# FFN inner and outer products on 32x32 places of TensorE, one expert to a place, without the mask

## Chip, cores and metric

One core of a Trainium2 chip. The metric is device time in microseconds, the median of the runs shown. Three runs of the kernel before took 2077.69 (median), 2072.56 and 2080.45 us. The profiled execution took 2074.38 us, of which the span from the first to the last instruction is 2072.3.

## What is computed

The input x is 10000 rows of 512. A graph layer comes first: layernorm, messages over 5000 edges summed by destination, two matrix products with batchnorm and silu, and the result added to x. The FFN follows, and the change is in it alone. Cut to what matters:

```python
grouped = x.reshape(B, S // t, t, D)                      # t = 16 tokens to a group, D = 512
cont_logits = einsum('bgtd,des->bgtes', grouped, controller) + tie
cont_perm = (cont_logits == max(cont_logits, over t))     # per group, each of 64 (e, s) picks one token
inner = einsum('bgtesf,bgtes->bgesf', einsum('bgtd,desf->bgtesf', grouped, f1), cont_perm)
inter2 = einsum('bgesf,esfd->bgesd', relu(inner), f2)     # f = 32
result = einsum('bgesd,bgtes->bgtd', inter2, cont_perm)
```

So 64 experts (16 x 4 pairs e, s) each take one token of every group of 16, multiply it by a 512x32 matrix of their own, take relu, multiply by a 32x512 matrix of their own, and give the sum back to that token. Everything is f32.

## The kernel before

The graph layer takes the first 1240 us or so and is untouched. The FFN walks the 10000 rows in 20 chunks of 512 tokens (the last has 272). A chunk has G = 32 groups. It goes through four steps of a pipeline, and `step` (L695) holds, for one turn, the work of four chunks in an order written by hand: chunk `a` is normalized and gets its logits and choice, chunk `b` gathers and does the inner product, chunk `d` the outer product, chunk `e` scatters to the output; `nxt` is the chunk that is loaded. A scheduler interleaves neighbours slightly (the first gather with the residual transposes, outer with the logits), and each engine then runs its own queue in order.

What the stages do in a turn, by line:

- `by_token` (L581) turns the choice of `b` into one-hot columns; DVE makes the mask `bd` from it (L587).
- `residual` (L523 to L526) and `norm` (L532 to L539) prepare rows of `a`; `flip` (L547, L549) transposes them, `logits` (L557) multiplies by the controller and `choose` (L570 to L573) finds the maxima on DVE.
- `gather(k)` (L602), for each quarter k of the 512 features, multiplies the normalized rows with the one-hot mask: for each expert and group, the chosen token's features, in the two `pb` buffers of PSUM. ACT copies both to `gs` (L608).
- `inner(k)` (L623) multiplies `gs` by f1. A stationary operand holds 64 columns, that is two experts of 32, and the moving operand the 64 columns of the same two experts' tokens (32 groups each). So each product has four blocks of 32x32, of which two are an expert with its own tokens and two are an expert with the other's tokens. Four k are summed in PSUM, in `pi`.
- `relu` (L630) takes relu of all of `pi` on DVE and multiplies by the mask `own` (1 for the wanted blocks, 0 for the others) into `ib`.
- `outer(u)`, u = 0 to 3 (L645), multiplies `ib` by f2: 64 rows (two experts) by 64 columns, on four places of the array. A half `i` of u fills one `pb` buffer, and is copied into `it` at once, by DVE (L651) for the first half of u = 0 and 1, by ACT (L653) for the others.
- `turn` (L659) is eight 32x32-wise transposes of `it` on DVE, `split` (L668) makes the scatter's mask on GpSimd, `scatter` (L686) multiplies both back to tokens, again in `pb`, and DVE adds the result to the rows (L692), which then go out.

[...]`ps` two of one bank, `pb` two buffers of two banks each, and `pi` one buffer of two banks, which the logits use too. The two `pb` buffers are handed round between gather, outer and scatter, so a matmul that takes a buffer waits for the copy or the addition that reads it last. f2 is loaded by eight DMAs before the first turn.

Of the kernel before, what the change touches and what calls it, by code (L numbers as in the profile page):

```python
# [35 lines left out]
G = CH // T  # L36
# [14 lines left out]
def gnn_ffn_kernel(ctx: ExitStack, tc: tile.TileContext, a: dict, out: bass.AP):  # L51
    nc = tc.nc
# [10 lines left out]
    const = ctx.enter_context(tc.tile_pool(name="const", bufs=1))  # L63
# [114 lines left out]
    with tc.tile_pool(name="pe1", bufs=1) as pe1, tc.tile_pool(name="pe", bufs=2) as pe, \  # L178
# [48 lines left out]
        for t in range(NTE):  # L227
            nc.gpsimd.indirect_dma_start(
                out=xgs[t], out_offset=None, in_=x,
# [3 lines left out]
        for g in range(NTE // EG):  # L233
# [9 lines left out]
            for i in range(EG):  # L243
                r = row[:, :i + 1, :]
                d = dst_f[:, g * EG + i:g * EG + i + 1]
# [3 lines left out]
                                               op0=ALU.is_equal, op1=ALU.mult, accum_out=count[:, i:i + 1])  # L249
# [21 lines left out]
            for i in range(EG):  # L271
                t = g * EG + i
# [6 lines left out]
            for i in range(EG):  # L279
                pc = ps_e.tile([TE, H], F32, name="pc", bufs=3)  # L280
                for k in range(i, EG):
                    nc.tensor.matmul(pc, lhsT=same[k][:, i, :], rhs=xgs[g * EG + k], start=(k == i),  # L282
                                     stop=(k == EG - 1))
                nc.scalar.copy(xgs[g * EG + i], pc)
                sums.append(tc.keep_in_program_order(nc.gpsimd.indirect_dma_start(
                    out=views[i], out_offset=bass.IndirectOffsetOnAxis(ap=to_i[:, i:i + 1], axis=0),
                    in_=xgs[g * EG + i], in_offset=None, compute_op=ALU.add)))
# [116 lines left out]
    with tc.tile_pool(name="pb", bufs=1) as pb, tc.tile_pool(name="ps_3", bufs=1, space=PSUM) as ps_3:  # L404
        u2 = weight_sums(pb, "w2", w2, 4, H // 2)
        for o, i in enumerate([NP - 1, *range(NP - 1)]):
            if o > 0:
# [4 lines left out]
                for m in range(4):  # L412
                    for r in range(2):
                        h = pieces[m][:, r].rearrange("p t n -> p (t n)")
                        nc.scalar.activation(h, h, AF.Silu, bias=sh1[:, 4 * r + m:4 * r + m + 1],
                                             scale=sc1[:, 4 * r + m:4 * r + m + 1])
            else:
                for r, t in ((0, 0), (1, 1), (1, 0), (0, 1)):
                    for m in range(4):
                        h = pieces[m][:, r, t, :]  # L420
# [3 lines left out]
            for m in range(2):  # L424
# [3 lines left out]
                for r in range(2):  # L428
                    for t in range(2):
                        nc.vector.bn_stats(out=st2[:, 2 * r + m, 2 * i + t, :], in_=h2[:, r, t, :])  # L430
                nc.sync.dma_start(out=h2s.rearrange("p (r m) n -> p m r n", r=2)[:, m, :, 2 * i * TB:2 * (i + 1) * TB],
                                  in_=h2.rearrange("p r t n -> p r (t n)"))
# [5 lines left out]
    ctl = const.tile([P, KH, 2, ES // 2], F32, name="ctl")  # L438
# [4 lines left out]
    for h in range(2):  # L443
        nc.sync.dma_start(out=tie[h * ES:(h + 1) * ES, :], in_=a["c_tie"])

    own = const.tile([P, 2, G], F32, name="own")
    nc.vector.memset(own, 0.0)
    for r in range(4):
        nc.vector.memset(own[32 * r:32 * r + 32, r % 2, :], 1.0)

    gmask = load_const("c_gmask", [P, 8])
    odd_p = const.tile([P, 2], F32, name="odd_p")
    nc.vector.tensor_reduce(odd_p, gmask.rearrange("p (q h) -> p h q", h=2), AX.X, ALU.add)
# [5 lines left out]
    HD = H // 2  # L459
    wf = ctx.enter_context(tc.tile_pool(name="wf", bufs=1))  # L460
    f1_sb = wf.tile([P, KH, ES * F], F32, name="f1_sb")
    f2_sb = wf.tile([P, MF, H], F32, name="f2_sb")
    pf = ctx.enter_context(tc.tile_pool(name="pf", bufs=2))
    ps_s = ctx.enter_context(tc.tile_pool(name="ps_s", bufs=2, space=PSUM))
    ps_b = ctx.enter_context(tc.tile_pool(name="ps_b", bufs=2, space=PSUM))
    ps_i = ctx.enter_context(tc.tile_pool(name="ps_i", bufs=1, space=PSUM))

    class Chunk:

# [82 lines left out]
        def logits(self, k, xlt):  # L552

            if k == 0:
                self.pl = ps_i.tile([P, 2, CH], F32, name="pi")
            for h, (o, n) in enumerate(self.halves):
                nc.tensor.matmul(self.pl[h * ES:(h + 1) * ES, 0, :n], lhsT=ctl[:, k].rearrange("p h j -> p (h j)"), rhs=xlt[:, o:o + n],  # L557
                                 start=(k == 0), stop=(k == KH - 1), skip_group_check=True)

        def choose(self):  # L560

            self.perm = pf.tile([P, CH // 2], F32, name="perm", bufs=5)
            mx = pf.tile([P, G // 2], F32, name="mx")
            if not self.full:
                nc.vector.memset(self.perm, 0.0)
            for s, n in [(slice(0, P), CH // 2)] if self.full else [
                    (slice(h * ES, (h + 1) * ES), n) for h, (_, n) in enumerate(self.halves)]:
                k, g = s.stop - s.start, n // T
                lg = self.perm[s, :n].rearrange("e (g t) -> e g t", t=T)
                nc.vector.tensor_add(lg, self.pl[s, 0, :n].rearrange("e (g t) -> e g t", t=T),  # L570
                                     tie[s, None, :].to_broadcast([k, g, T]))
                nc.vector.tensor_reduce(mx[s, :g], lg, AX.X, ALU.max)
                nc.vector.tensor_tensor(lg, lg, mx[s, :g, None].to_broadcast([k, g, T]), ALU.is_equal)  # L573
# [39 lines left out]

        def inner(self, k, gs):


            if k == 0:
                self.pi = ps_i.tile([P, MF, 2 * G], F32, name="pi")
            gs = gs.rearrange("p (h j) g -> p h j g", h=2)
            for m in range(MF):  # L620
                for q in range(2):
                    j = 4 * (m // 2) + 2 * q + m % 2
                    nc.tensor.matmul(self.pi[64 * q:64 * q + 64, m, :], lhsT=f1_sb[:, k, 2 * F * j:2 * F * (j + 1)],  # L623
                                     rhs=gs[:, :, j, :],
                                     start=(k == 0 and m % 8 == 0), stop=(k == KH - 1), skip_group_check=True)

        def relu(self):

            self.ib = pf.tile([P, MF, 2 * G], F32, name="ib")
            nc.vector.scalar_tensor_tensor(self.ib, self.pi, 0.0, own.rearrange("p h g -> p (h g)")[:, None, :]  # L630
                                           .to_broadcast([P, MF, 2 * G]), op0=ALU.max, op1=ALU.mult)

        def outer(self, u):


            if u == 0:
                self.it = pf.tile([P, HD // 2, 32, 2], F32, name="it", bufs=1)
            for i in range(2):
                b = 2 * u + i
                po = ps_b.tile([P, 2, 2, HD], F32, name="pb")  # L640
                for t in range(2):
                    for dh in range(2):
                        for q in range(2):
                            s = slice(64 * q, 64 * q + 64)
                            nc.tensor.matmul(po[64 * dh:64 * dh + 64, q, t, :], lhsT=self.ib[s, 2 * b + t, :],  # L645
                                             rhs=f2_sb[s, 2 * b + t, HD * dh:HD * (dh + 1)], start=True, stop=True,
                                             skip_group_check=True)
                dst = self.it[:, :, 4 * b:4 * b + 4, :].rearrange("p d c l -> p c d l")
                src = po.rearrange("p q t (d l) -> p (q t) d l", l=2)
                if i == 0 and u < 2:  # L650
                    nc.vector.tensor_copy(dst, src)  # L651
                else:
                    nc.scalar.copy(dst, src)  # L653
# [128 lines left out]
        chunks[c].silu()  # L782
    nc.sync.dma_start(out=f1_sb, in_=a["L0_ffn_f1"].rearrange("(k p) n -> p k n", p=P))

    f2 = a["L0_ffn_f2"].rearrange("(b q t h f) d -> q h f b t d", h=2, q=2, t=2, f=F)
    f2_to = f2_sb.rearrange("p (b t) d -> p b t d", t=2)
    for q in range(2):
        for h in range(2):
            for t in range(2):
                rows = slice(64 * q + F * h, 64 * q + F * (h + 1))  # L790
                nc.sync.dma_start(out=f2_to[rows, :, t, :], in_=f2[q, h, :, :, t, :])
    for c in range(NC + 3):
        step(at(c), at(c - 1), at(c - 2), at(c - 3), at(c + 1))

# [60 lines left out]
```

## Time and profile before

| | us |
|---|---|
| median of three runs | 2077.69 |
| profiled execution | 2074.38 |
| its span | 2072.3 |
| graph layer, to the FFN's first chunk choice | about 1270 |
| FFN turns with all four chunks, most of them | 37.0 to 37.2 each |
| PE busy in the turn from 1500 to 1537 | 35.06 |
| DVE, ACT, GpSimd busy there | 22.13, 18.93, 9.81 |
| mean granted TensorE clock, whole span | 0.948 |

In a profile row of a group, the columns are line, engine, operation, output and inputs by name, then the count, the busy time, the mean duration of one in ns, and the idle time before it with what ended it. A row of the timeline has the start in us, the length of the merged stretch, then engine and line, the count, and in square brackets the idle time before it with its cause. A row of windows has, for each engine, busy time and number of instructions, then the granted clock, the share of the DMA engines and GB/s. Busy times of PE overlap, since matmuls on different places of the array run at once; so the distance between starts says more than the duration of one.

### The profile page before, as it was taken

The numbers are of one execution on the slowest core, as the hardware profiler recorded it, in microseconds if no ns is written. First come the engines' busy times: TensorE is split into PE (matmuls) and PEld (weight loads), VectorE is DVE, ScalarE is ACT, GpSimd is POOL, SyncE is SP. The second block draws the span as 40 slices with busy tenths as digits, with TensorE's granted clock in tenths as the row PEclk, the third lists the DMA queues.
The fourth block names the chain that finished last, engine by engine and source line by source line (L and its number), as shares of the span: only waits on it lengthen the run. The fifth ranks groups of instructions, "written<-read, shape, count | busy, mean of one in ns | idle before, by whom it ended". The sixth has DMA issues, their size and how long they took to land.

```text
span 2072.3 us, 38292 instructions
## 1 busy us (share of the span) xinstructions
PE 1858.1 (90%) x16562; PEld 1041.7 (50%) x16562; DVE 1145.5 (55%) x1860; ACT 726.4 (35%) x969; POOL 626.7 (30%) x630
## 2 busy tenths in 40 slices
PE   7935499999999989999999996899989999999984
PEld 3412244444444434444444444576666676666662
DVE  9723267777777774334333442265565565665655
ACT  3412233333333333222222203454454554545422
POOL 7144433333333324222233313023222122222311
PEclk9967699999999999999999997899999999999987
DMA  9986444444444122322333209222222222222110
GB/s 354 359 176 87 110 181 157 160 161 159 161 160 160 80 80 119 139 119 119 126 132 120 118 40 253 73 83 76 91 83 94 75 82 94 93 75 83 34 39 35
DMA packets 95119, 256.01 MB, mean 124 GB/s; under 512 B 7767, under 2 KB 8357, under 8 KB 94374
## 3 DMA queue, kind: packets, MB, share of 16 engines
q1 hardware_dynamic: 85990, 232.58, 30.7%
q0 software_dynamic: 8960, 20.98, 5.0%
q8 instruction: 130, 2.13, 0.4%
q14 instruction: 39, 0.32, 0.0%
HBM read 143.47 MB, written 110.07 MB: 122 GB/s over the span
## 4 chain that ended last, share of the span: by engine, by line
PE 66%; DVE 13%; DMA 7%; ACT 6%; POOL 5%; issue 3%; SPq 0%; DVEq 0%; POOLq 0%; ACTq 0%
PE x L133 9%; PE z L133 9%; PE pi L623 7%; PE pb L645 7%; PE v L133 5%; PE w L133 5%; PE pb L602 5%; PE pb L686 4%; PE pc L282 3%; PE y L133 3%; PE pi L557 2%; DVE ln_st L329 2%; DMA yt<-h2s 2%; ACT xt L341 2%; PE pt L133 2%
## 5 line engine op out<-in xcount | busy, mean ns | idle before, releaser
L133 PE MATMUL x<-h_s,w_u 128*128 128x500 f32 x640 | 289.5, 585 | 0.6 <-ACT s L138 0.3
L653 ACT COPY it<-pb 128x1024 f32<-128x1024 f32 x120 | 121.8, 1050 | 256.5 <-PE pb L645 256.5
L645 PE MATMUL pb<-f_sb,ib 64*64 64x256 f32 x2560 | 191.1, 390 | 11.1 <-DVE x L692 8.4
L133 PEld LDWEIGHTS x<-h_s,w_u 128*128 128x128 f32 x640 | 122.3, 191 | 148.8 <-issue 142.4
L659 DVE STREAM_TRANSPOSE it<-it 128x1024 f32<-128x1024 f32 x160 | 186.9, 1212 | 11.3 <-ACT it L653 11.3
L608 ACT COPY gs<-pb 128x1024 f32<-128x1024 f32 x152 | 153.1, 1065 | 101.6 <-PE pb L602 101.6
L623 PE MATMUL pi<-gs,f_sb 128*64 128x64 f32 x5120 | 178.5, 232 | 5.2 <-issue 5.2
L623 PEld LDWEIGHTS pi<-gs,f_sb 128*64 128x64 f32 x5120 | 167.4, 146 | 20.6 <-issue 14.1
L602 PE MATMUL pb<-bd,xl 32*128 32x128 f32 x2504 | 143.6, 302 | 35.8 <-ACT gs L608 26.9
L668 POOL TENSOR_TENSOR pv<-perm,odd_t 64x512 f32<-64x512 f32 (+1 forms) x80 | 99.7, 1246 | 222.0 <-PE pb L686 194.1
L133 PE MATMUL z<-h_s,w 128*128 128x500 f32 x320 | 148.0, 585 | 3.3 <-POOL h_s L123 3.3
L143 DVE SCALAR_TENSOR_TENSOR t<-w,s 128x500 f32<-128x500 f32 x60 | 40.7, 678 | 190.5 <-PE w L133 186.7
L602 PEld LDWEIGHTS pb<-bd,xl 32*128 32x128 f32 x2504 | 115.4, 196 | 60.7 <-ACT gs L608 38.8
L133 PE MATMUL z<-h_s,w_u 128*128 128x500 f32 x320 | 143.9, 583 | 0.0
L645 PEld LDWEIGHTS pb<-f_sb,ib 64*64 64x64 f32 x2560 | 95.3, 134 | 88.6 <-issue 29.7
L123 POOL TENSOR_TENSOR h_s<-hc 128x500 f32<-128x500 f32 x60 | 77.0, 1319 | 148.7 <-PE z L133 148.7
L532 POOL TENSOR_SCALAR ln_rs<-ln_mv 128x4 f32<-128x4 f32 (+2 forms) x22 | 4.9, 224 | 373.4 <-DVE ln_mv L526 363.7
L138 ACT COPY s<-z 128x500 f32<-128x500 f32 x60 | 34.5, 575 | 219.2 <-PE z L133 150.2
L692 DVE TENSOR_TENSOR x<-pb,x 128x1024 f32<-128x1024 f32 (+1 forms) x40 | 48.2, 1208 | 101.9 <-PE pb L686 101.9
L686 PE MATMUL pb<-it,pv 64*32 64x256 f32 x2504 | 81.7, 395 | 20.8 <-DVE it L659 20.8
L348 PE MATMUL pt<-ident,xt 125*128 125x125 f32 x320 | 47.9, 288 | 56.6 <-DVE xt L342 47.8
L341 ACT ACTIVATE xt<-xt,ln_sh,ln_rs 125x512 f32<-125x512 f32 x80 | 59.6, 805 | 110.4 <-POOL ln_sh L336 110.4
(174 smaller groups left out, 3078.8 us busy)
## 6 DMA issues: line engine op xcount, KB each, us to landing
h1s<-h SPq DMA_DIRECT2D x36, 1000.0 KB
agg<-zero SPq DMA_DIRECT2D x10, 2048.0 KB
xt<-in_x_dram SPq DMA_DIRECT2D x20, 1000.0 KB
at<-agg SPq DMA_DIRECT2D x20, 1000.0 KB
hc<-h1s SPq DMA_DIRECT2D x20, 1000.0 KB
h2s<-h SPq DMA_DIRECT2D x20, 1000.0 KB
x<-in_x_dram SPq DMA_DIRECT2D x39, 512.0 KB
out_dram<-x SPq DMA_DIRECT2D x39, 512.0 KB
```

Of the source, the lines that this page charges most:

```text
L123: eng.tensor_tensor(t[:, k0:k1], q(*x0, k0, k1), q(*x1, k0, k1), op)
L133: nc.tensor.matmul(bank, lhsT=us[n][:, k, m * P:(m + 1) * P], rhs=bs[n][k], start=start and k == 0, stop=k == kb - 1, skip_group_check=True)
L282: nc.tensor.matmul(pc, lhsT=same[k][:, i, :], rhs=xgs[g * EG + k], start=(k == i), stop=(k == EG - 1))
L341: nc.scalar.activation(r, r, AF.Identity, bias=self.sh[:RT, j, :], scale=self.rs[:RT, j, :])
L602: nc.tensor.matmul(pg[r // 2][:, r % 2, j], lhsT=self.xl[j][s, k * P:(k + 1) * P], rhs=self.bd[s, j], start=True, stop=True)
L608: nc.scalar.copy(to[:, 8 * i:8 * i + 8], pg[i].rearrange("d r j e h -> d (r j) e h"))
L623: nc.tensor.matmul(self.pi[64 * q:64 * q + 64, m, :], lhsT=f1_sb[:, k, 2 * F * j:2 * F * (j + 1)], rhs=gs[:, :, j, :], start=(k == 0 and m ...
L645: nc.tensor.matmul(po[64 * dh:64 * dh + 64, q, t, :], lhsT=self.ib[s, 2 * b + t, :], rhs=f2_sb[s, 2 * b + t, HD * dh:HD * (dh + 1)], start ...
L653: nc.scalar.copy(dst, src)
L659: nc.vector.transpose(it, it)
L668: nc.gpsimd.tensor_tensor(self.pv[dh * ES:(dh + 1) * ES, :, o:o + n].rearrange("e v (q t) -> e v q t", q=q), self.perm[i * ES:(i + 1) * ES ...
L686: nc.tensor.matmul(pr[32 * r:32 * r + 32, dh, j % 2, :], lhsT=self.pv[s, v, tok], rhs=self.it[s, :, 2 * (4 * r + j) + v, :], start=(v == 0 ...
```

## The change

Inner and outer work on one expert at a time, 32 rows and 32 columns each. `inner` issues 64 matmuls per k instead of 32, each with 32 stationary and 32 moving columns, on the four column places in turn; no product of an expert with another's tokens is formed, so the mask `own` is gone, `relu` is a plain maximum over half as many elements, and `pi` is half as wide. `pi` is one bank now and has two buffers. `outer(u)` issues 32 matmuls instead of 16, on 16 places (four of rows, four of columns), takes both `pb` buffers at its start and fills their four banks, one bank to a row place; the innermost loop goes over the row places, so every second pair of matmuls is in the second buffer. After all 32, DVE copies the first buffer and ACT the second, for every u. The rows of f2 are laid out to fit, by 16 DMAs of half the size.

```diff
-    own = const.tile([P, 2, G], F32, name="own")
-    nc.vector.memset(own, 0.0)
-    for r in range(4):
-        nc.vector.memset(own[32 * r:32 * r + 32, r % 2, :], 1.0)
...
-    ps_i = ctx.enter_context(tc.tile_pool(name="ps_i", bufs=1, space=PSUM))
+    ps_i = ctx.enter_context(tc.tile_pool(name="ps_i", bufs=2, space=PSUM))
...
-                self.pl = ps_i.tile([P, 2, CH], F32, name="pi")
+                self.pl = ps_i.tile([P, CH], F32, name="pi")
...
             if k == 0:
-                self.pi = ps_i.tile([P, MF, 2 * G], F32, name="pi")
-            gs = gs.rearrange("p (h j) g -> p h j g", h=2)
+                self.pi = ps_i.tile([P, MF, G], F32, name="pi")
+            gs = gs.rearrange("p (h j) g -> p j h g", h=2)
             for m in range(MF):
-                for q in range(2):
-                    j = 4 * (m // 2) + 2 * q + m % 2
-                    nc.tensor.matmul(self.pi[64 * q:64 * q + 64, m, :], lhsT=f1_sb[:, k, 2 * F * j:2 * F * (j + 1)],
-                                     rhs=gs[:, :, j, :],
-                                     start=(k == 0 and m % 8 == 0), stop=(k == KH - 1), skip_group_check=True)
+                for r in range(4):
+                    j, h = 8 * (m // 4) + 2 * r + m % 4 // 2, m % 2
+                    nc.tensor.matmul(self.pi[32 * r:32 * r + 32, m, :], lhsT=f1_sb[:, k, F * (2 * j + h):F * (2 * j + h + 1)],
+                                     rhs=gs[:, j, h, :], start=(k == 0 and m == 0), stop=(k == KH - 1),
+                                     skip_group_check=True)
...
-            self.ib = pf.tile([P, MF, 2 * G], F32, name="ib")
-            nc.vector.scalar_tensor_tensor(self.ib, self.pi, 0.0, own.rearrange("p h g -> p (h g)")[:, None, :]
-                                           .to_broadcast([P, MF, 2 * G]), op0=ALU.max, op1=ALU.mult)
+            self.ib = pf.tile([P, MF, G], F32, name="ib")
+            nc.vector.tensor_scalar(self.ib, self.pi, 0.0, None, op0=ALU.max)
...
+            po = [ps_b.tile([P, 2, 2, HD], F32, name="pb") for _ in range(2)]
+            for t in range(2):
+                for h in range(2):
+                    for dh in range(2):
+                        c = 64 * dh + 32 * h
+                        for r in range(4):
+                            s = slice(32 * r, 32 * r + 32)
+                            m = 4 * u + 2 * t + h
+                            nc.tensor.matmul(po[r // 2][c:c + 32, r % 2, t, :], lhsT=self.ib[s, m, :],
+                                             rhs=f2_sb[s, m, HD * dh:HD * (dh + 1)], start=True, stop=True,
+                                             skip_group_check=True)
             for i in range(2):
-                b = 2 * u + i
-                po = ps_b.tile([P, 2, 2, HD], F32, name="pb")
-                for t in range(2):
-                    for dh in range(2):
-                        for q in range(2):
-                            s = slice(64 * q, 64 * q + 64)
-                            nc.tensor.matmul(po[64 * dh:64 * dh + 64, q, t, :], lhsT=self.ib[s, 2 * b + t, :],
-                                             rhs=f2_sb[s, 2 * b + t, HD * dh:HD * (dh + 1)], start=True, stop=True,
-                                             skip_group_check=True)
-                dst = self.it[:, :, 4 * b:4 * b + 4, :].rearrange("p d c l -> p c d l")
-                src = po.rearrange("p q t (d l) -> p (q t) d l", l=2)
-                if i == 0 and u < 2:
+                dst = self.it[:, :, 8 * u + 4 * i:8 * u + 4 * i + 4, :].rearrange("p d c l -> p c d l")
+                src = po[i].rearrange("p q t (d l) -> p (q t) d l", l=2)
+                if i == 0:
                     nc.vector.tensor_copy(dst, src)
                 else:
                     nc.scalar.copy(dst, src)
...
-    for q in range(2):
-        for h in range(2):
-            for t in range(2):
-                rows = slice(64 * q + F * h, 64 * q + F * (h + 1))
-                nc.sync.dma_start(out=f2_to[rows, :, t, :], in_=f2[q, h, :, :, t, :])
+    for u in range(4):
+        for r in range(4):
+            nc.sync.dma_start(out=f2_sb[32 * r:32 * r + 32, 4 * u:4 * u + 4, :], in_=f2[u, r])
```

More of the change, by code (lines that the diff above doesn't have):

```diff
@@ L554, in logits @@
             if k == 0:
-                self.pl = ps_i.tile([P, 2, CH], F32, name="pi")
+                self.pl = ps_i.tile([P, CH], F32, name="pi")
             for h, (o, n) in enumerate(self.halves):
-                nc.tensor.matmul(self.pl[h * ES:(h + 1) * ES, 0, :n], lhsT=ctl[:, k].rearrange("p h j -> p (h j)"), rhs=xlt[:, o:o + n],
-                                 start=(k == 0), stop=(k == KH - 1), skip_group_check=True)
+                nc.tensor.matmul(self.pl[h * ES:(h + 1) * ES, :n], lhsT=ctl[:, k].rearrange("p h j -> p (h j)"),
+                                 rhs=xlt[:, o:o + n], start=(k == 0), stop=(k == KH - 1), skip_group_check=True)
         def choose(self):
@@ L569, in choose @@
                 lg = self.perm[s, :n].rearrange("e (g t) -> e g t", t=T)
-                nc.vector.tensor_add(lg, self.pl[s, 0, :n].rearrange("e (g t) -> e g t", t=T),
+                nc.vector.tensor_add(lg, self.pl[s, :n].rearrange("e (g t) -> e g t", t=T),
                                      tie[s, None, :].to_broadcast([k, g, T]))
@@ L783, in gnn_ffn_kernel @@
     nc.sync.dma_start(out=f1_sb, in_=a["L0_ffn_f1"].rearrange("(k p) n -> p k n", p=P))
-    f2 = a["L0_ffn_f2"].rearrange("(b q t h f) d -> q h f b t d", h=2, q=2, t=2, f=F)
-    f2_to = f2_sb.rearrange("p (b t) d -> p b t d", t=2)
-    for q in range(2):
-        for h in range(2):
-            for t in range(2):
-                rows = slice(64 * q + F * h, 64 * q + F * (h + 1))
-                nc.sync.dma_start(out=f2_to[rows, :, t, :], in_=f2[q, h, :, :, t, :])
+    f2 = a["L0_ffn_f2"].rearrange("(u r b f) d -> u r f b d", u=4, r=4, f=F)
+    for u in range(4):
+        for r in range(4):
+            nc.sync.dma_start(out=f2_sb[32 * r:32 * r + 32, 4 * u:4 * u + 4, :], in_=f2[u, r])
     for c in range(NC + 3):
```

## The prediction

> **What bounds the kernel now.** I read the page, then one step of the FFN stage in order of time, then its windows, and last the single matmul records. The page puts PE on top, with the two lines that the change rewrites:
>
> ```profile
> PE 1858.1 (90%) x16562; PEld 1041.7 (50%) x16562; DVE 1145.5 (55%) x1860; ACT 726.4 (35%) x969; POOL 626.7 (30%) x630
> ...
> L645 PE MATMUL pb<-f_sb,ib 64*64 64x256 f32 x2560 | 191.1, 390 | 11.1 <-DVE x L692 8.4
> ...
> L623 PE MATMUL pi<-gs,f_sb 128*64 128x64 f32 x5120 | 178.5, 232 | 5.2 <-issue 5.2
> ```
>
> Inner (L623) and outer (L645) hold PE for 370 us. Every f32 matmul of the program stands in the trace as two, so I count passes. A full step lasts 37.0 to 37.2 us in most of its turns. The timeline of the one from 1499.82 to 1536.84 shows what ends each wait of PE:
>
> ```profile
> 1508.51 2.04 ACT L608 COPY gs<-pb 128x1024 f32<-128x1024 f32 x2
> ...
> 1509.63 0.49 PE L602 MATMUL pb<-bd,xl 32*128 32x128 f32 x4 [0.55 <-ACT gs L608]
> 1510.61 1.16 PE L602 MATMUL pb<-bd,xl 32*128 32x128 f32 x28 [0.48 <-ACT gs L608]
> 1511.70 2.08 PE L623 MATMUL pi<-gs,f_sb 128*64 128x64 f32 x64
> 1511.85 2.11 ACT L608 COPY gs<-pb 128x1024 f32<-128x1024 f32 x2
> 1513.71 1.45 PE L602 MATMUL pb<-bd,xl 32*128 32x128 f32 x32
> 1515.10 2.09 PE L623 MATMUL pi<-gs,f_sb 128*64 128x64 f32 x64
> 1517.11 1.96 PE L686 MATMUL pb<-it,pv 64*32 64x256 f32 x64
> 1521.02 1.96 PE L686 MATMUL pb<-it,pv 64*32 64x256 f32 x64
> 1522.91 1.09 PE L645 MATMUL pb<-f_sb,ib 64*64 64x256 f32 x16
> 1523.09 1.22 DVE L692 TENSOR_TENSOR x<-pb,x 128x1024 f32<-128x1024 f32 x1 [0.73 <-PE pb L686]
> 1524.37 1.09 PE L645 MATMUL pb<-f_sb,ib 64*64 64x256 f32 x16 [0.36 <-DVE x L692]
> ```
>
> PE is full but for about 1 us at 1509 to 1511: gather(2) waits for the ACT copies that free the two pb buffers. Gather(3) starts at 1513.71 and needs the copy that ends at 1513.96. So the first two inners run in the shade of ACT. Inner(2) and inner(3) do not, and outer doesn't either.
>
> The last view is the clock. Two windows, the second with one drop to half speed:
>
> ```profile
> 1500.00:1537.00 37.00, 35.06 (x691) 24.96 (x691) 22.13 (x30) 18.93 (x23) 9.81 (x12) 1.00 0.27 88
> 1537.00:1574.00 37.00, 32.80 (x644) 24.34 (x647) 20.85 (x27) 16.08 (x20) 9.81 (x12) 0.95 0.28 87
> ```
>
> That step took 40.55 us.
>
> **How matmuls pack.** In the records, passes on different places of the array start 6 to 7 ns apart, then a gap follows until the places are free: L623 starts two in 58.5 ns, L645 four in 216, L686 eight in 218. A full-array 128x500 pass takes 418 ns, so a column costs 0.83 ns, and 64 columns 53, 256 columns 213. Each round is one stream plus about 5 ns.
>
> **The change, part by part, for one full step.**
> - Inner: 128 passes of 32 columns per k, four column places. A stream is 27 ns, four starts 26. A round is about 33 ns, 32 rounds make 1.05, and with the 0.15 that lies between a block's rounds and the next block 1.2 us; now it is 2.01 (1515.10 to 1517.11). Gain 0.8 each. For inner(0) and inner(1) it is nothing: gather(2) and (3) wait for ACT in any case. For inner(2) and (3) it is 1.6.
> - Is that rate sustained? The Trainium skill ("TensorE: Matmul & The Clock Gate", Part 1, section "Wait — 56ns, not 53.3ns?") says that starts never come closer than about 25 ns. By that, an inner takes 128 x 25 = 3.2 us and the change loses. Against it stand the rounds of 6 to 7 ns, but L686 averages 25 ns, so no row shows more than a burst. In L686's later rounds, the last weight loads come 17 ns apart for every two passes, as if just decoded: 8.5 ns a pass. I take that (34 ns a round) and keep 25 for the range.
> - Outer: 64 passes per u on 16 places instead of 32 on four. Four rounds of 218 would be 0.87. But L686's late loads read as a queue of about 64 entries; 16 places with two passes, each a load and a matmul, fill it, and the second half comes late. I take 1.4 us, between 0.87+0.2 and the present 1.88 (1532.49 to 1534.37).
> - Both pb buffers at once. The program's order has the third matmul of outer(u) on the second buffer, so all wait for both evictions. Outer(0): now 2.48 from start to flips (two halves of 1.05 and the wait); then 1.25 (L692 after scatter(1)) + 1.4 = 2.65, +0.15. Outer(1), with flips and lo(0): 4.2 becomes 3.9, -0.3. Outer(2): 4.8 becomes 4.3, -0.5. Outer(3): lo(3) covers 0.6 of the 1.4 that a DVE copy (1.22) takes to come free, so lo(3), 0.8 of stall and 1.4 of work, and by_token 0.15 later for choose: 2.95 against 2.47, +0.5.
> - Evictions: of the eight copies of a step DVE takes four instead of two (1.22 each, from L651's rows), ACT four instead of six (1.05, L653). One has a victim: DVE's copy of outer(3) now stands between choose and bd. bd (now 0.48 after by_token) waits till about 1.3, and the first gather with it: +0.8.
> - relu: half as wide, 1.23 to about 0.65. It ends while scatter(1) runs, so nothing. Were scatter(1) gone, it would be worth 0.6. The second pi buffer takes away DVE's hold on logits, 0.5 us in all. The five dropped memsets lie under the start of the GNN stage.
> - Loads: 16 DMAs of 256 KB instead of 8 of 512: 8 x 0.4 us more on SP's queue, before loads of chunk 2 that come 40 us later; nothing, at worst 3 us.
> - Instruction stream: 24,242 passes instead of 16,562, so about 190 fetches of 16 KB instead of 130 (0.9 to 1.6 us each). At 1287 to 1292 PE once waits 5.2 us at "issue" while the weights load; I put +3 there (0 to 6).
>
> Sum per step: -1.6 +0.15 -0.3 -0.5 +0.5 +0.8 = -0.95.
>
> **The clock.** I added up, for each 3.41 us window between 1365 and 1950, columns x 0.83 ns x the share of the array that a pass covers. Of 168 windows at full speed three are followed by half speed, with shares 0.14, 0.22, 0.25; the lowest that is not has 0.37. Half-speed windows that end at once have 0.75 or more (half of it is again 0.37), those that are followed by another 0.72 or less. So the bar is on work, about 0.37. The change takes away products with zeros: the work of inner and outer halves (13.6 to 6.8 of 25.7 us per step, the mean share falls from 0.69 to about 0.51). The window around gather(2) has about 1.5 us of work now (0.43). Afterwards it holds inner(0)'s 0.85 and gather(2)'s first 0.1 to 0.2: 0.3 and less, for most positions of the window. I expect one drop per step in place of one in five, and sometimes a second window. The Trainium skill (same page, section "Why this matters for your kernels") asks only for no idle gap over about 3 us; by that, the stalls here (under 2 us) cost nothing and the step is 0.95 faster. The rows decide: the three drops came after stalls of 2 to 3.3 us.
> Price: those steps took 39.28, 40.55 and 39.81. Less 37.1 and the longer stall itself (1.0, 2.3, 1.5) each leaves 1.2. With 0.3 for second windows: +1.5 per step.
>
> **Sum.** 17 full steps x (-0.95 + 1.5) = +9. Two filling steps gain at inner: -3. In two draining steps outer has no filler; a u there takes 1.4 + 1.4 = 2.8 instead of 2.3, and the wait for L692 comes on top: +7 for both with a slow clock. Fetching +3. Together +16 on 2074.38 (span 2072.3 and 2.1 around it): 2090. The median of the three runs is 3.3 higher, so I say 2092.
>
> **Rivals.**
> - *Packs as in bursts, clock stays up* (the other side). Outer takes 1.1, inner 1.1, and the stall stays above the bar. The step is -0.95 -0.2 -0.9 = -2.05, 17 x that is -35, filling -3, draining and fetching +6: about 2045. For it: the 6 to 7 ns starts. Against: the work that vanishes. It decides where the drops cost less than 0.95 per step.
> - *PE cannot be fed.* 25 ns a pass: inner 3.35 instead of 2.0, +1.35 x 4 less 0.7 that the stall at gather(2) takes; outer as long as now but with both buffers, +2.1 with bd's delay. +6.8 per step, 17 of them +115, and the rest: about 2210. The work share falls too, so it can be more.
> - *The low clock sticks.* A half-speed window with outer's late second half or a stall has under 0.72 and is followed by another: +3 per step in place of 1.5, about 2125.
>
> **Numbers.** The likeliest case 0.50, alone 2070 to 2110; packs well 0.22; sticks 0.18; cannot be fed 0.10. Within 0.5% is about what a measurement can tell from no change: 2067 to 2088. Faster is most of the second case and a little of the first: 0.24; same: the lower part of the first: 0.21; slower 0.55. Range 2043 to 2150; it leaves out cannot-be-fed and the tails.
>
> **What would show it.** Inner's 128 passes in 1.1 to 1.2 us; gather(2) waiting 0.8 longer for L608; outer(0) with a pause after its first four passes, for L692; outer(3) waiting 0.8 for the DVE copy; bd 0.8 later; granted clock of the stage near 0.90 in place of 0.99. I am wrong if inner's starts average over 15 ns, if the clock's bar is not on work, or if the share of half-speed windows stays where it is.

## The result, and the profile after

| | before | after |
|---|---|---|
| median, us (4 runs each, in turn) | 2075.12 | 2176.49 |
| lowest and highest | 2069.07 to 2080.45 | 2167.59 to 2180.37 |
| ratio, 95% interval | | 1.0483 [1.0435, 1.0532] |
| profiled execution, its span | 2074.38, 2072.3 | 2167.59, 2165.6 |

The changed kernel is 4.8% slower, outside the range of the prediction. Its page, for the rows of PE (TensorE; DVE is VectorE, ACT is ScalarE) and the queue that brings the instructions (48,484 weight loads and matmuls of PE, 190 transfers of 16 KB, so 255 to each):

```profile
PE 1829.8 (84%) x24242; PEld 984.8 (45%) x24242; DVE 1183.8 (55%) x1895; ACT 689.6 (32%) x929; POOL 626.5 (29%) x630
...
q8 instruction: 190, 3.11, 0.6%
...
L639 PE MATMUL pb<-f_sb,ib 32*32 32x256 f32 x5120 | 176.6, 411 | 28.9 <-ACT it L648 19.1
...
L617 PE MATMUL pi<-gs,f_sb 128*32 128x32 f32 x10240 | 125.6, 209 | 62.6 <-issue 62.5
...
L681 PE MATMUL pb<-it,pv 64*32 64x256 f32 x2504 | 101.1, 424 | 49.9 <-issue 28.7
```

Read the two columns behind the bars against each other. Inner (now L617) is busy for 126 us where it was busy for 179, as it should be. But the idle time ahead of it is 62.6 us where it was 5.2, and scatter (now L681), which the change doesn't touch, has 28.7 us of the same kind. The cause is given as "issue": PE waited for nothing that the profile shows.

The waits of PE from the first choice of the FFN to the end, first after, then before (us in total, times, longest):

```profile
PE pi L617 <- issue: 62.5, 43, 5.3
PE pb L597 <- ACT gs L603: 35.7, 52, 1.7
...
PE pb L681 <- issue: 28.7, 17, 2.6
...
PE pb L597 <- DVE bd L582: 17.0, 19, 1.4
...
PE pb L597 <- issue: 5.2, 7, 1.4
```

```profile
PE pb L602 <- ACT gs L608: 26.9, 46, 2.8
...
PE pb L686 <- DVE it L659: 20.8, 2, 10.4
PE pb L645 <- DVE x L692: 8.4, 19, 1.6
PE pi L623 <- issue: 5.2, 1, 5.2
...
PE pb L602 <- DVE bd L587: 4.2, 18, 0.9
```

All rows of "issue" in this stretch add up to 98.8 us after and 6.5 before. The difference, 92.3, is as large as the whole growth of the span (93.3). By parts of the FFN, cut at the one-hot columns (`by_token`) of the first, fourth and nineteenth chunk:

| | before, us | after, us | issue before | issue after |
|---|---|---|---|---|
| filling, first to fourth | 115.2 | 133.1 | 6.5 | 28.1 |
| 15 full turns | 564.5 | 635.4 | 0 | 62.5 |
| the rest | 121.6 | 127.8 | 0 | 8.2 |

One turn of after in order of time, with the granted clock at full speed all through:

```profile
1495.06 1.30 PE L617 MATMUL pi<-gs,f_sb 128*32 128x32 f32 x128
1497.90 0.49 PE L597 MATMUL pb<-bd,xl 32*128 32x128 f32 x4 [1.54 <-ACT gs L603]
...
1499.93 1.30 PE L617 MATMUL pi<-gs,f_sb 128*32 128x32 f32 x128
...
1503.36 1.41 PE L617 MATMUL pi<-gs,f_sb 128*32 128x32 f32 x128
1504.70 1.06 PE L681 MATMUL pb<-it,pv 64*32 64x256 f32 x22
1507.53 1.51 PE L681 MATMUL pb<-it,pv 64*32 64x256 f32 x42 [1.76 <-issue]
1508.97 0.95 PE L617 MATMUL pi<-gs,f_sb 128*32 128x32 f32 x86
1511.00 0.57 PE L617 MATMUL pi<-gs,f_sb 128*32 128x32 f32 x42 [1.08 <-issue]
1511.50 1.97 PE L681 MATMUL pb<-it,pv 64*32 64x256 f32 x64
1513.39 1.04 PE L639 MATMUL pb<-f_sb,ib 32*32 32x256 f32 x18
1514.85 1.71 PE L639 MATMUL pb<-f_sb,ib 32*32 32x256 f32 x46 [0.41 <-DVE x L687]
```

Each inner does take 1.3 us, about as forecast (1.2). Then PE stops in the middle of scatter(0), and again in the middle of inner(3), at a place where no operand changes. Count the passes between the two stops: 42 of scatter and 86 of inner are 128. A pass is a weight load and a matmul, so that is 256 instructions, as many as one transfer on the instruction queue brings. In the records of that queue such transfers start at 1501.22, 1504.79 and 1508.65 and take 0.9 to 1.3 us. PE goes on at 1507.53 and 1511.00, some 1.4 us after the second and the third one had ended.

This holds for the whole trace. Number PE's instructions in order (weight loads, matmuls and semaphore instructions) and divide by 256. All 60 of its pauses over 0.5 us that are put down to issue in the FFN have the remainder 193 or 194, the border between two blocks. In the kernel with inner(3) four times (below) it is 109 of 109, with 193 to 195.

So theory F: PE gets its instructions in blocks of 256, a block comes only every 3 to 4 us, and a dense stretch uses what lies ready and then waits. Rival C is the clock, which has 18 drops to half speed in the 15 turns where there were 3 before. Rival B is outer: its two buffers at once, and DVE's copies. A last one is the decoder: small passes start further apart than the bursts in the trace of before had shown.

### The profile page after: what moved, and what is told of

Same layout as the page of the kernel before. It is cut to its first block, busy times and chain, and to the rows that moved or that the text cites. A ratio compares the mean times of both kernels' runs of the same rounds, so it can differ in the third digit from the quotient of the medians.

```text
span 2165.6 us, 53675 instructions
## 1 busy us (share of the span) xinstructions
PE 1829.8 (84%) x24242; PEld 984.8 (45%) x24242; DVE 1183.8 (55%) x1895; ACT 689.6 (32%) x929; POOL 626.5 (29%) x630
## 4 chain that ended last, share of the span: by engine, by line
PE 61%; DVE 13%; issue 8%; ACT 8%; DMA 6%; POOL 5%; another core or an unknown queue 0%; SPq 0%; DVEq 0%; POOLq 0%; ACTq 0%
PE x L133 9%; PE z L133 9%; PE pb L639 7%; PE pb L597 5%; PE v L133 5%; PE w L133 5%; PE pb L681 5%; PE pi L617 4%; PE y L133 3%; PE pc L282 3%; ACT gs L603 2%; DVE ln_st L329 2%; ACT it L648 2%; PE pi L552 2%; ACT xt L341 2%
## 5 line engine op out<-in xcount | busy, mean ns | idle before, releaser
L597 PE MATMUL pb<-bd,xl 32*128 32x128 f32 x2504 | 154.3, 319 | 61.7 <-ACT gs L603 35.7
L639 PE MATMUL pb<-f_sb,ib 32*32 32x256 f32 x5120 | 176.6, 411 | 28.9 <-ACT it L648 19.1
L648 ACT COPY it<-pb 128x1024 f32<-128x1024 f32 x80 | 82.8, 1035 | 362.9 <-PE pb L639 362.9
L603 ACT COPY gs<-pb 128x1024 f32<-128x1024 f32 x152 | 154.2, 1070 | 126.5 <-PE pb L597 126.4
L617 PE MATMUL pi<-gs,f_sb 128*32 128x32 f32 x10240 | 125.6, 209 | 62.6 <-issue 62.5
L646 DVE COPY it<-pb 128x1024 f32<-128x1024 f32 x80 | 98.0, 1225 | 144.3 <-PE pb L639 144.3
L597 PEld LDWEIGHTS pb<-bd,xl 32*128 32x128 f32 x2504 | 122.8, 211 | 88.0 <-ACT gs L603 49.4
L617 PEld LDWEIGHTS pi<-gs,f_sb 128*32 128x32 f32 x10240 | 111.3, 120 | 85.8 <-issue 80.5
L681 PE MATMUL pb<-it,pv 64*32 64x256 f32 x2504 | 101.1, 424 | 49.9 <-issue 28.7
L687 DVE TENSOR_TENSOR x<-pb,x 128x1024 f32<-128x1024 f32 (+1 forms) x40 | 48.3, 1209 | 168.2 <-PE pb L681 168.2
L639 PEld LDWEIGHTS pb<-f_sb,ib 32*32 32x32 f32 x5120 | 81.4, 106 | 103.3 <-ACT it L648 37.6
```

The source lines that it names most:

```text
L597: nc.tensor.matmul(pg[r // 2][:, r % 2, j], lhsT=self.xl[j][s, k * P:(k + 1) * P], rhs=self.bd[s, j], start=True, stop=True)
L603: nc.scalar.copy(to[:, 8 * i:8 * i + 8], pg[i].rearrange("d r j e h -> d (r j) e h"))
L617: nc.tensor.matmul(self.pi[32 * r:32 * r + 32, m, :], lhsT=f1_sb[:, k, F * (2 * j + h):F * (2 * j + h + 1)], rhs=gs[:, j, h, :], start=(k ...
L639: nc.tensor.matmul(po[r // 2][c:c + 32, r % 2, t, :], lhsT=self.ib[s, m, :], rhs=f2_sb[s, m, HD * dh:HD * (dh + 1)], start=True, stop=True ...
L681: nc.tensor.matmul(pr[32 * r:32 * r + 32, dh, j % 2, :], lhsT=self.pv[s, v, tok], rhs=self.it[s, :, 2 * (4 * r + j) + v, :], start=(v == 0 ...
```

## The experiments

"Issue" and "low clock" below are for the 15 full turns of the profiled execution: the idle time of PE that is put down to issue, per turn, and the sum of the time at half speed. The turn is the mean of the 15. A ratio is to runs of the kernel before that were taken beside the kernel in its row, so it is not the quotient of two medians of this table.

| kernel | median, us | ratio to before, 95% | turn, us | issue per turn | low clock |
|---|---|---|---|---|---|
| before | 2075.12 | | 37.63 | 0 | 10.2 |
| after | 2176.49 | 1.0483 [1.0435, 1.0532] | 42.36 | 4.17 | 78.5 |
| inner alone | 2148.08 | 1.0388 [1.0366, 1.0409] | 41.12 | 3.68 | 64.9 |
| outer alone | 2076.98 | 1.0043 [1.0019, 1.0067] | 37.57 | 0 | 3.4 |
| after, outer in halves | 2172.98 | 1.0524 [1.0475, 1.0573] | 41.89 | 4.41 | 75.1 |
| after, useless matmul | 2162.40 | 1.0464 [1.0433, 1.0494] | 42.10 | 4.63 | 51.2 |
| outer alone, bd free | 2067.57 | 0.9982 [0.9968, 0.9996] | 37.02 | 0 | 3.4 |
| new inner(0), (1) | 2103.52 | 1.0152 [1.0114, 1.0189] | 38.79 | 0.63 | 64.9 |
| new inner(2), (3) | 2136.69 | 1.0328 [1.0283, 1.0372] | 40.29 | 3.09 | 30.7 |
| the same for (0), (1), with matmul | 2098.59 | 1.0122 [1.0097, 1.0147] | 38.33 | 0.83 | 10.2 |
| outer, bd free, new inner(3) | 2083.15 | 1.0051 [1.0031, 1.0070] | 37.57 | 1.11 | 6.8 |
| after, spread | 2178.47 | 1.0522 [1.0493, 1.0551] | 43.12 | 3.31 | 146.8 |
| after, inner(3) four times | 2388.95, one run | | 53.92 | 9.47 | 259.4 |
| outer alone, old inner(3) four times | 2178.65, one run | | 43.49 | 0.05 | 23.9 |

### Which half of the change

Inner alone, on the kernel before (`pi` is halved and has two buffers, as in after, and relu masks in two operations; not shown):

```diff
-                for q in range(2):
-                    j = 4 * (m // 2) + 2 * q + m % 2
-                    nc.tensor.matmul(self.pi[64 * q:64 * q + 64, m, :], lhsT=f1_sb[:, k, 2 * F * j:2 * F * (j + 1)],
-                                     rhs=gs[:, :, j, :],
+                for r in range(4):
+                    j, h = 4 * (m // 2) + 2 * (r // 2) + m % 2, r % 2
+                    nc.tensor.matmul(self.pi[32 * r:32 * r + 32, m, :], lhsT=f1_sb[:, k, F * (2 * j + h):F * (2 * j + h + 1)],
+                                     rhs=gs[:, h, j, :],
```

> Inner in its new form (64 matmuls of 32 columns per k), outer as before (64x64 places, half by half); relu masks in two operations. If the loss comes from PE running out of instructions where two inners of 256 instructions stand among scatters (theory F), the stalls at inner(2), scatter(0) and inner(3) stay: 1.5 to 3 us per step of issue idle on PE against inner's gain of 1.6, so 2070 to 2110. If it comes from outer's two buffers and DVE's copies (theory B), this kernel keeps inner's gain and loses nothing: 2040 to 2060. If from the clock (theory C), it has about half the additional drops: about 2085.

Outer alone, with the 64-column inner (the experts renumbered so that it needs no mask; `pi` stays one buffer of two banks, not shown):

```diff
-                for r in range(4):
-                    j, h = 8 * (m // 4) + 2 * r + m % 4 // 2, m % 2
-                    nc.tensor.matmul(self.pi[32 * r:32 * r + 32, m, :], lhsT=f1_sb[:, k, F * (2 * j + h):F * (2 * j + h + 1)],
-                                     rhs=gs[:, j, h, :],
+                for q in range(2):
+                    j, t, h = 8 * (m // 4) + 4 * q, m % 4 // 2, m % 2
+                    e = 32 * h + j + 2 * t
+                    j = j + t
+                    nc.tensor.matmul(self.pi[64 * q:64 * q + 64, m, :], lhsT=f1_sb[:, k, F * e:F * (e + 2)],
+                                     rhs=gs[:, h, j:j + 3:2, :],
```

> Outer in its new form (16 places, both buffers), inner as before with 64 columns; relu without a mask but full width; the experts are numbered differently so that both fit. F: hardly any issue stalls, so what is left is the buffers' and copies' price, 2080 to 2105. B: nearly the whole loss, over 2140. C: about half of the additional drops, 2090 to 2100.

After, with outer's copies and buffers in two halves as before:

```diff
-            po = [ps_b.tile([P, 2, 2, HD], F32, name="pb") for _ in range(2)]
...
             for i in range(2):
+                po = ps_b.tile([P, 2, 2, HD], F32, name="pb")
...
+                            for r in range(2 * i, 2 * i + 2):
...
-                if i == 0:
+                if i == 0 and u < 2:
```

> The changed kernel with outer in two halves again (8 places of 32x32 each, one pb buffer at a time, copies divided as before). B: the outer stalls and the later bd go, 1.0 to 1.5 us per step less, but outer itself takes 1.75 instead of 1.4: 2150 to 2165 by F, which says that inner's issue stalls stay (1.5 to 3 us per step); by B alone below 2110.

Inner alone costs 77.6 us over the median of its call (2070.47), outer alone 6.5: 84 of the 101 that both cost together; what the other 17 come from, no run here takes apart. The page of inner alone has the pauses, in inner and again in the untouched scatter:

```profile
L623 PE MATMUL pi<-gs,f_sb 128*32 128x32 f32 x10240 | 127.6, 210 | 59.7 <-issue 59.6
...
L687 PE MATMUL pb<-it,pv 64*32 64x256 f32 x2504 | 94.4, 409 | 49.0 <-issue 26.4
```

Outer alone has one, while the weights load, as before has:

```profile
PE pi L621 <- issue: 4.0, 1, 4.0
```

It issues 2560 passes more than before, and none of its full turns pauses. More instructions alone do no harm; it matters where they stand. Outer in halves changes nothing that can be told: its interval overlaps that of after. So B is not the cause. F's own times were too low, though: at most 2110 for inner alone and 2165 for outer in halves, where 2148.1 and 2173.0 were measured.

### The clock, or the instructions

A full-array matmul whose result nobody reads, after inner(0), to keep the work up where the clock drops:

```diff
         inn(0)
+        if b and b.full:
+            idle = ps_s.tile([P, H], F32, name="ps")
+            tc.keep_in_program_order(nc.tensor.matmul(idle, lhsT=ident, rhs=g0.rearrange("p e g -> p (e g)")[:, :H], start=True, stop=True))
         turns(2, 4)
```

> The changed kernel with one useless full-array 128x512 matmul (two passes of 427 ns) after inner(0), in the gap in which PE waits for ACT; its result is not read. C: the windows around gather(2) rise from 0.25 to 0.5 of the array's work, drops in the FFN stage go from 19 to under 10, each worth 1.2 us: 12 to 25 us faster, about 2155. F: instructions hardly change, issue idle stays near 90 us, and the time stays within 10 us of the changed kernel's.

The drops in the 15 turns fell from 18 to 10, the low clock from 78.5 to 51.2 us, and the turn only from 42.36 to 42.10: PE waited 0.46 more for issue. The time can't be told from after's, since the intervals overlap. At about 1.0 us for a drop, as the pair for k < 2 below gives, all 18 are 18 us. The clock is not what cost 100 us.

The decisive pair is next. After, with inner(3) issued four times:

```diff
-        inn(3)
+        if b:
+            gs3 = b.gs.pop(3)
+            for _ in range(4):
+                b.inner(3, gs3)
```

> The changed kernel with inner(3) issued four times in a row, so that the last quarter of the features is counted four times. The disputed rate by itself: 512 passes (1024 instructions) with nothing else for PE to do. If the array and the decoder set the rate (8.5 ns a pass, as in the first inner's records), the three added inners cost 3 x 1.1 = 3.3 us per step. If PE gets a block of 256 instructions only every 2.7 us (the distance from a fetch's start to PE's going on in the changed kernel), each added inner costs 2.7 us, 8 us per step, with pauses at every 128th pass: some 160 us on the whole kernel.

And the control, the same edit on outer alone, whose inner has 64 passes of 64 columns:

> The control to the run with the new inner(3) four times: the new outer layer with the old inner (64 passes of 64 columns), and its inner(3) issued four times (the last quarter of the hidden layer is counted four times). The old form uses its 64 passes in 2.0 us, so 256 instructions in 4.0 us, just slower than the 3.7 us that a block of 256 takes. Theory F: no pauses for issue in the full steps, each added inner(3) costs 2.0 us, so 20 chunks by 3 by 2.0 = 120 us over 2077, 2197, and less than the new form's 2389. Rival, repeated work on TensorE costs more for another reason (the filling of the same banks, the clock): each added one costs 3 us or more, 2257 or later, with or without issue pauses.

A turn of the first, at inner(3):

```profile
1498.88 0.31 PE L617 MATMUL pi<-gs,f_sb 128*32 128x32 f32 x11
1499.70 1.28 PE L617 MATMUL pi<-gs,f_sb 128*32 128x32 f32 x128 [0.51 <-issue]
1503.72 1.28 PE L617 MATMUL pi<-gs,f_sb 128*32 128x32 f32 x128 [2.74 <-issue]
1507.19 1.93 PE L617 MATMUL pi<-gs,f_sb 128*32 128x32 f32 x128 [2.19 <-issue]
1510.93 1.82 PE L617 MATMUL pi<-gs,f_sb 128*32 128x32 f32 x117 [1.81 <-issue]
```

A turn of the control, at the same place:

```profile
1537.98 1.96 PE L685 MATMUL pb<-it,pv 64*32 64x256 f32 x64
1539.87 7.69 PE L621 MATMUL pi<-gs,f_sb 128*64 128x64 f32 x256
1547.49 1.96 PE L685 MATMUL pb<-it,pv 64*32 64x256 f32 x64
```

The new form runs 128 passes, stops, runs 128 passes, stops. With nothing around it, it shows its own period: six transfers of instructions from 1497.52 to 1516.40 start 3.78 us apart. The old form runs its 256 passes, which are two blocks, in 7.69 us without a stop. Per added inner the new form costs (53.92 - 42.36) / 3 = 3.85 us, and the old form (43.49 - 37.57) / 3 = 1.97. One block for 128 passes, half a block for 64. The form without useless products costs twice as much when it stands by itself. F's figure was too low, and the decoder's more so (1.1 us). F had taken 2.7 us a block, from the start of a transfer to PE's going on; that leaves out the time before a transfer starts. F's size is 3.8 us a block. The decoder falls as the cause: within a block the passes start 8.7 ns apart.

The records show what the 3.8 us are made of. In this kernel's full turns 86 blocks were waited for. In the median, the transfer of a block started 1.14 us after PE's first instruction of the block before it, took 1.12, and PE went on 1.38 after its end: 3.64 in sum. So one block is fetched ahead, and only when PE comes to the one in front of it (158 of 171 transfers start after that one's first instruction, the others at most 1.1 us before it). A block that PE runs through in less than some 3.7 us is followed by a wait for the rest.

### Where dense passes may stand

Five kernels on outer alone. First the one copy that delays `bd` is moved to ACT:

```diff
-                if i == 0:
+                if i == 0 and u < 3:
```

> The kernel with the new outer and the old inner, with both copies of outer(3) on ACT, so that DVE's bd does not stand behind a copy. B: bd comes 0.8 us earlier, 17 steps, 10 to 14 us faster than with the new outer alone, about 2063 and faster than before. If the gathers wait for the second pb buffer in its place (ACT's second copy ends 0.9 us later than DVE's did), nothing is gained: 2077.

Then outer alone with the new inner only for k < 2, or only for k >= 2 (`if k < 2:` ahead of the 32-column loop, the 64-column loop otherwise):

> New outer; inner(0) and inner(1) in the new form, inner(2) and (3) in the old one. F: their 256 instructions each are issued where PE afterwards waits for ACT in any case, so a pause for instructions there hides behind that wait: within 10 us of the new outer alone (2067 to 2090). If the new inner itself is the cost, wherever it stands (a slower rate of small passes, or the clock), half of the 78 us that the new inner cost alone: about 2115.

> New outer; inner(2) and (3) in the new form, (0) and (1) in the old one. F: the pauses stand in front of the scatters, where nothing hides them, and eat more than the 1.6 us that the new form saves: 2090 to 2130, with issue idle of 20 to 50 us at inner and scatter. If the rate were the cost wherever it stands: as with the other two, 2115. If there were no fetch limit, 2050.

The free `bd` makes the turn 0.55 us shorter than outer alone, and this version is the one that is faster than the kernel before, if only by 0.2% (22 runs of it, the interval ends at 0.9996). The two mixed kernels issue as many instructions of each kind, and yet the waits in the whole trace are:

```profile
PE pi L622 <- issue: 17.9, 13, 4.6
```

for k < 2, and for k >= 2:

```profile
PE pi L622 <- issue: 38.9, 27, 5.3
PE pb L695 <- issue: 25.6, 18, 2.3
```

From inner(2) to the end of outer(0) the second issues 448 passes in what would be some 8.9 us of work, and 3.5 blocks need 13.3. The first has 320 passes there, 2.5 blocks or 9.5 us, and takes 10.7 for them (1486.40 to 1497.08 in one turn). Its dense passes stand beside PE's waits for ACT. In the full turns it pauses 0.63 us each, and yet is 1.2 us longer than outer alone; so F does not explain all of it: it had said 2090 at most (and 2130 for k >= 2). The low clock is the suspect there, and was tried with the useless matmul after inner(0) in that kernel:

> The new inner for k below 2 only (2103.5 before), plus one useless full-array 128x512 matmul after inner(0), where TensorE waits 1.5 us for the scalar engine's copy. Theory C: in that kernel the steps are 1.2 us longer than with the outer layer alone although TensorE hardly waits for instructions there (26 us of issue idle, most of it while the pipeline fills), because the clock is low for 65 us in the full steps; the useless matmul fills the array, the low-clock time falls below 30 us, the steps fall from 38.8 to under 38.1 us and the time to 2085 to 2093. Rival F alone: the steps stay at 38.5 to 39 us and the time at 2100 to 2110, with the low clock gone or not.

The windows of k < 2 without and with the matmul (the granted clock is the number after POOL):

```profile
1395.00:1970.00 575.00, 506.55 (x14098) 358.03 (x14090) 361.24 (x476) 251.29 (x295) 147.00 (x180) 0.94 0.25 82
```

```profile
1395.00:1970.00 575.00, 510.93 (x14222) 348.13 (x14220) 367.72 (x486) 252.90 (x297) 146.99 (x180) 0.99 0.25 82
```

Ten drops of 13 are gone, and the turn is 0.46 us shorter, with 0.20 more of issue. Its time, 2098.6, lies between what C and F gave. If the added issue is taken out, ten drops were worth 15 x 0.66 = 9.9 us: 1.0 each. The filler's own cost is in that, so it may be a little more. The 0.8 that is left over outer alone is about the 0.83 of issue.

New inner for k = 3 alone, on the version with `bd` free (`if k == 3:`):

> The new outer layer with both copies of outer(3) on the scalar engine (2067.6 before) and the new inner for k = 3 alone. Theory F with little lying ready: the saved 0.8 us of each step is lost, since inner(3), scatter(1) and outer(0) now use 512 instructions in 5 us, which two blocks at 3.7 us can't bring: issue idle of 20 to 40 us, time 2070 to 2095. Rival, a block or two lie ready and carry one dense inner: no pauses in the full steps, each step 0.8 us shorter, time 2050 to 2058, the fastest of all.

```profile
1516.04 1.06 PE L622 MATMUL pi<-gs,f_sb 128*32 128x32 f32 x101
1518.01 0.44 PE L622 MATMUL pi<-gs,f_sb 128*32 128x32 f32 x27 [0.90 <-issue]
```

Even one dense inner is not carried by what lies ready: the pause of 0.90 stands inside it, the turn pauses 1.11 us where 0.8 was to be saved, and the turn grows by 0.55.

Last, after with the flips and logits put between the dense pieces (the lines taken out further down are left out here):

```diff
         inn(2)
+        fl(0)
+        fl(1)
         put(e, Chunk.scatter, 0)
+        lo(0)
+        fl(2)
         inn(3)
         put(b, Chunk.relu)
+        lo(1)
...
```

> The changed kernel with sparse work put between its dense stretches: the flips and logits of the next chunk stand between inner(2), scatter(0), inner(3) and scatter(1) instead of among the passes of outer. Nothing is added or left out. Theory F (instructions come in blocks of 256, one block in about 3.7 us where they are used as fast as they come, and a dense stretch uses up what lies ready): the stretch from inner(2) to scatter(1) becomes some 6 us longer at the same number of passes, so the idle time of TensorE put down to issue falls from 118 us to 50 to 70, and the time from 2176 to 2110 to 2135. Rival, each block costs the same wherever it stands: issue idle stays within 15 us of 118 and the time at 2165 to 2185. Rival C (the clock): the time follows the share of low clock and the issue idle doesn't fall.

The waits of PE in it, full turns:

```profile
PE ps L542 <- POOL xl L534: 69.9, 13, 5.4
PE pi L617 <- issue: 33.5, 33, 2.4
PE pb L681 <- issue: 10.6, 12, 1.6
```

Issue fell from 98.8 us in the FFN to 79.1, in the full turns from 62.5 to 49.7. The 118 of the expectation holds 19.4 us of a single wait in the graph layer, which this trace puts down to DVE; so the fall is 20 us, less than half of what F had said. The scheduler also pulled the first flips ahead of gather(1), where GpSimd's rows are not ready yet: a new wait of 69.9 us, and nearly twice the low clock. So this order trades one wait for another. The direction is what F said, the time is what its rival said (2165 to 2185), and the run decides nothing. Whether an order exists that spreads the passes without such a wait stays open.

## Why the prediction was wrong

The direction was right, the mechanism of nearly all of the loss was not. Point by point:

- *Inner, 1.2 us instead of 2.01*: right. Where nothing interrupts it, it takes 1.23 to 1.49 to the next start, 8.7 ns a pass. The starts come 7 ns apart within a round for the first 35 passes or so and then two in 17 ns, which fits the queue of about 64 entries that the prediction reads from L686.
- *Inner(0) and (1) gain nothing*: right for the path. Gather(2) waits 1.54 for L603 where it waited 0.55.
- *Outer*: right. Outer(1) takes 3.76 us (3.9), outer(2) 4.29 (4.3), outer(3) 2.74 (2.95); outer(0) 3.1 for 2.65 in after, but 2.73 in the version with outer alone and `bd` free, which has no pauses. The pause for L687 (0.41) is where it should be. Outer(3) waits 0.56 for ACT's copy, where 0.8 for DVE's was forecast.
- *bd +0.8*: right. The first gather starts 1.78 after `by_token` where it started after 1.04, and moving the copy to ACT gave back 0.55 of the turn.
- *Clock, one drop per turn or a few more at 1.2 us*: right in count (18 in 15 turns) and about in price (1.0 each by the pair above). The bar is on the work done in the array, as said: all windows of after's full turns that were followed by half speed had a share under 0.30. That some windows between 0.26 and 0.31 stayed at full speed shows that 0.37 was too high for a sharp bar. The mean clock of the full turns was 0.94, not 0.90.
- *The sum per turn, -0.95 + 1.5 = +0.55*: after's turn less its pauses is 42.36 - 4.17 = 38.19, +0.56 over before. Part of that is luck, since a pause can hide another wait, so the subtraction is not exact. (The last step of the total, 2090 and 3.3 more, makes 2093 and not 2092; nothing hangs on it.)
- *"I put +3 there (0 to 6)"*, for the instruction stream: this is the step that failed. The count of 190 fetches instead of 130 was right to the digit. The price was taken from the only pause that the trace of before shows, one of 5.2 us while the weights load, as if fetching was a matter of how many there are and not of how close together they are used. It measured 92 us more: 62.5 in the full turns, 21.6 in the filling turns, and the other 8.2 while the pipeline drains. In the filling turns the forecast had a gain of 3, and blocks start up to 6.6 us apart there while PE waits for them, beside the loads of f1 and f2. The Trainium skill ("Runtime: NRT & Kernel Launch", section "Instruction fetch mechanics") describes the same blocks of 256 instructions, and calls the cost of a block mostly hidden, because instructions are issued more slowly than they are brought. Here it is the other way round: 8.7 ns a pass is 4.3 ns an instruction, and 3.8 us a block is 15 ns an instruction. The measurement decides.

The rival "PE cannot be fed" (0.10, 2210) had the right place and came closest in time, by another mechanism: it spaced all starts by the 25 ns of the Trainium skill ("TensorE: Matmul & The Clock Gate", Part 1, section "Wait — 56ns, not 53.3ns?"). The trace shows neither that nor an endless 8.5: it is 8.7 ns a pass as long as instructions lie ready, and 3.8 us / 128 = 30 ns a pass after that. Before's 64-column inner takes 2.01 / 64 = 31 ns a pass, just slower than the supply. So the kernel before stood close to the limit. In its FFN PE takes 3.86 us or more for every block, and in its full turns no block is used sooner than 1.92 us after its transfer has ended. In after's, 61 of 126 are used within 1.6 us, none sooner than 1.20.

The trace of before could have bounded it. In its FFN fetches start at least 3.44 us apart, and in the turn that the prediction shows (1508 to 1523) every 4.3 to 5.2 us. A change that puts 256 instructions into 1.2 us asks for three times as much, and nothing in the trace said that this could be had. The range should have taken the 3.4 us per block as the other end: 448 passes from inner(2) to outer(0) are 3.5 blocks, 12 us for 8.9 us of work, 3.1 us per turn or 53 in 17.

## What to carry to other kernels

Count instructions per stretch of time, not only per kernel: here TensorE was brought 256 instructions, 128 f32 passes with their loads, every 3.8 us, and what a dense stretch needs beyond that it waits for, in whatever matmul comes next. A split of matmuls into smaller ones that wins by the array's work can lose by that, so look for the smallest distance between instruction fetches in the trace before and compare it with what the change would ask for (passes in a stretch / 128 x 3.8 us against the stretch's time here); "issue" in front of an untouched instruction is the sign afterwards. Here dense passes were cheapest where the engine waits for others anyway (k < 2), and there they brought nothing either, except a lower clock.

## What was not expected of the hardware

- In none of the 14 traces do two 16 KB fetches of PE's instructions start less than 3.23 us apart, though one takes 0.9 to 2.0 us, and in after the queue is busy 0.6% of the DMA engines' time. The rest of the period is waiting: 1.14 us in the median until the next transfer starts and 1.38 after it has ended, in the kernel with inner(3) four times.
- While instructions lie ready, f32 passes of 32 columns on four places of the array start 8.7 ns apart in the mean for 128 in a row.
- A matmul of no use that filled the array kept the clock up (0.94 to 0.99) at a net gain of 0.46 us per turn.
